# A graph-convolution kernel: the last unit takes the first two row tiles of g from SBUF instead of gathering them

## The chip, the cores and the metric

The kernel runs on one NeuronCore of one Trainium2 chip. The metric is the device time of one launch in microseconds, as the median of several runs. The inputs are fixed: the adjacency matrix always has the same pattern of zeros, so the sizes of all lists below are the same in every run.

## The reference

```python
# x: (8, 4096, 256), adj: (4096, 4096), W: (256, 256), all float32
HW = einsum('bnf,fo->bno', x, W)
A = relu((adj + adj.T) * 0.5)                 # sparse: most entries are 0
D = A.sum(1);  d = where(D > 0, D ** -0.5, 0)
out = relu(einsum('nm,bmo->bno', I - d[:, None] * A * d[None, :], HW))
result = layernorm(x + out)                   # over the last axis, eps 1e-5
```

An entry of adj off the diagonal is nonzero with a probability that falls with row and column number, so the first rows of A are the densest.

## The kernel before, in words

*Stage one* symmetrises adj in blocks of 512, writes A with an altered diagonal to a tensor in DRAM (`a_dram`), forms g = d * x * W (one row of g has all 8 batches, 2048 numbers or 8 KB) and writes it to `g_dram`. It also marks, for every row of A and every group of 32 columns, whether the row has any entry there (`uses`). Row tile 0 of the output is computed in this stage.

*Stage two* computes the other 31 row tiles of 128 rows, in units: unit u makes row tiles 2u+1 and 2u+2, its two blocks, and unit 15, the last, only row tile 31. The order of units is `SEQ`. Most rows of A have no entry in a given block, so a unit does not multiply with all 4096 rows. From the marks the kernel builds lists on the device (`patterns`, `place`, `index`, on VectorE, with a few small products on TensorE): which rows have entries in which of the eight groups of 32 columns. A list is cut into tiles of 128 entries, in two halves of 64 slots. `FIRST` and `CAPS` say for each unit and each kind of row (one group only, several groups, and so on) at which half the kind's slots begin and how many halves it has; the number of list tiles of a unit follows from them. A row of a one-group kind that finds no slot goes to a kind for several groups; a row that finds none at all would send the whole program into a slow branch with dense products, which these inputs do not reach.

For each list tile two indirect DMAs on GpSimd's queue (L951, L959) gather the entries of A (tile `ga`, 128 rows by 32, 128 or 256 columns) and the rows of g (tile `g`, 128 by 2048, 1 MB; rows of g are skipped for blank slots). They go into a ring of 12 slots, in the order of first use; a slot is refilled when TensorE has used its tile for the last time.

The first two row tiles of g, where A is dense, are kept in SBUF for the whole stage (`g_hub`, the hub tiles). `HUBS[u]` says how many of them unit u uses. `patterns` clears the marks of these rows (L262), so they do not enter the unit's lists. What they need is only a 128 by 128 piece of A for each block (`gh`), loaded with a plain DMA on GpSimd's queue by `load_hub_rows` as soon as the unit before has used its own.

Products are in *steps* (`steps_of`). A full step multiplies one 128 by 128 piece with 2048 columns of g: four matmuls of 512 columns into four PSUM banks. A tiled step uses TensorE as eight tiles of 64 by 32: `REACH` or `RING` list tiles are looked at, and for each bank up to eight products of different halves and column groups run at once. After the products of each bank of a tiled step, an empty instruction on ScalarE (L1201, a "tick") marks that they are done, and two banks later TensorE waits for it[...]. Tiles of rows with several groups in one block take a full step.

Behind the products of a block, `finish` evicts its four banks on ScalarE (L767), and VectorE adds x (L777), takes the statistics (L786, L788), forms the inverse root (L799 to L805) and scales (L810); SyncE stores. Row tile 31 has its own version, `finish_last`, which works in four quarters of two batches: evictions on ScalarE (L1016), adds on GpSimd (L1024, L1037) and VectorE (L1026, L1032), statistics on VectorE, the power on GpSimd (L1039), the scaling on ScalarE (L1048), four stores (L1055). The x it needs is loaded into the first ring slot that is free when all gathers have been asked for (L979). The order on each queue is the order in which the program is written: `queue(...)` ties a new instruction behind the last one of that engine, and `after(n, ...)` puts a piece of work some steps later.

The last unit before: `HUBS[15]` is 0, its list has ten tiles, and its steps are: one full step with list tile 8; two tiled steps with tiles 0, 2, 4, 6 and 1, 3, 5, 7, eight products a bank; one tiled step with tile 9, four products a bank. Unit 14 before it takes 11 steps; the last two are full steps of row tile 30 (hub tile 1 and a list tile), and the two before those are tiled steps in which row tile 29 ends.

Of the kernel before, what the change touches and what calls it, by code (L numbers as in the profile page):

```python
# [22 lines left out]

SEQ = [*range(1, 10), 0, *range(10, 16)]

HUBS = [*[2] * 15, 0]

CAPS = [
    [3, 4, 3, 3, 3, 2, 3, 3, 2, 3, 3, 3, 3, 3, 11],
# [11 lines left out]
    [2, 2, 2, 2, 3, 3, 3, 2, 2, 1, 1, 1, 1, 1, 1],  # L41
    [2, 2, 2, 2, 2, 2, 2, 2, 2, 2, 1, 1, 1, 1, 1],
    [2, 2, 2, 2, 2, 2, 2, 2, 2, 2, 1, 1, 1, 1, 1],
    [3, 4, 4, 4, 4, 0, 0, 0, 0, 0, 0, 0, 0, 0, 0],
]

FIRST = [
# [12 lines left out]
    [0, 2, 6, 4, 8, 16, 12, 21, 19, 15, 24, 28, 26, 25, 27],  # L60
    [2, 4, 6, 8, 0, 16, 18, 10, 14, 12, 20, 22, 21, 24, 23],
    [2, 6, 0, 4, 8, 14, 10, 16, 12, 18, 22, 24, 23, 20, 21],
    [16, 0, 4, 8, 12, 20, 20, 20, 20, 20, 20, 20, 20, 20, 20],
]


# [1 line left out]
def kernel(  # L68
# [49 lines left out]
    def blocks(u):  # L118

        return min(2, NB - 1 - 2 * u)  # L120
# [75 lines left out]
    singles, pairs, whole = slice(1, 1 + NE), slice(10, 14), slice(0, 10, 9)  # L196
# [28 lines left out]
    for s in range(NE):  # L225
        h = slice((s % QU) * E, (s % QU + 1) * E)
# [16 lines left out]
    def patterns(u):  # L243

        def t(shape, name, dtype=F32, **kw):
            return ipool.tile(shape, dtype, tag=name, name=f"{name}_{u}", **kw)
# [13 lines left out]
        nc.vector.tensor_tensor(diag, diag, own[:, :, :nb], ALU.max)  # L260
        if HUBS[u]:
            nc.vector.memset(used[:, :, : HUBS[u]], 0.0)  # L262
        several = t([P, NB], "several", bufs=1)
# [206 lines left out]
    with (  # L470
# [71 lines left out]
        held = {}  # L542
# [155 lines left out]
        for i in range(NS):  # L698
# [35 lines left out]
            if i in (1, 2, 3, 4):  # L734
                u = SEQ[i - 1]
# [6 lines left out]
            if i in (2, 4):  # L742
                u = SEQ[i // 2 - 1]
# [82 lines left out]
    def steps_of(u):  # L826

        kind_at = {}
        for k, kind in enumerate(KINDS):
            for s in range(FIRST[u][k], FIRST[u][k] + CAPS[u][k]):  # L830
                kind_at[s] = kind
        every = 255 if blocks(u) == 2 else 15
        whole = {0: [], 15: [], 240: []}
        todo = []
        for t in range(tiles[u]):
            pair = kind_at.get(2 * t), kind_at.get(2 * t + 1)
            if pair[0] == pair[1] and pair[0] in whole:
                whole[pair[0]].append(t)
                continue
            todo.append(  # L840
                [
                    (t, i, b, j)
                    for b in range(2)
                    for i, kind in enumerate(pair)
                    for j in range(QU)
                    if kind is not None and (kind or every) >> QU * b + j & 1
                ]
            )
        rounds = []
        while any(todo):  # L850
            todo = [ops for ops in todo if ops]
            taken = {}
            for ops in todo[: REACH if blocks(u) == 2 else RING]:
                for op in ops:
                    taken.setdefault((op[1], op[3]), op)
            rounds.append(list(taken.values()))
            todo = [[op for op in ops if op not in rounds[-1]] for ops in todo]
        n = len(rounds)
        first_b1 = min([r for r in range(n) if any(op[2] for op in rounds[r])], default=n)
        last_b0 = max([r for r in range(n) if any(not op[2] for op in rounds[r])], default=-1)  # L860

        def full(t, b):
            return [(t, None, b, None)]

        def weave(*several):
            several = [list(s) for s in several]
            total = [len(s) for s in several]
            out = []
            while any(several):
                at = max(range(len(several)), key=lambda k: (len(several[k]) / max(total[k], 1), total[k]))  # L870
                out.append(several[at].pop(0))
            return out

        held = range(HUBS[u])
        out = [full(-1, 0)] if HUBS[u] else []
        starts = [full(t, 0) for t in whole[15]]
        if not out and starts:
            out.append(starts.pop(0))
        out += weave(rounds[:first_b1], [full(-1 - h, 0) for h in held[1:]], starts)
        if blocks(u) == 1:  # L880
            return out + [full(t, 0) for t in whole[0]]
        out += [full(-1, 1)] if HUBS[u] else []
        rows = [[full(t, 0), full(t, 1)] for t in whole[0]]
        between = [[r] for r in rounds[first_b1 : max(last_b0 + 1, first_b1)]]
        out += chain.from_iterable(weave(between, rows))
        out += weave(
            [full(-1 - h, 1) for h in held[1:]],
            [full(t, 1) for t in whole[240]],
            rounds[max(last_b0 + 1, first_b1) :],
        )  # L890
        return out

    with (
# [5 lines left out]
            gath.enter_context(tc.tile_pool(name=f"hub_{h}", bufs=1)).tile([P, G], F32, name=f"g_hub{h}")  # L899
            for h in range(max(HUBS))  # L900
        ]
# [8 lines left out]
        lpool = gath.enter_context(tc.tile_pool(name="spread", bufs=1))  # L910
        stat = gath.enter_context(tc.tile_pool(name="stat", bufs=3))
        steps = [(u, step) for u in SEQ for step in steps_of(u)]
        order = list(dict.fromkeys((u, op[0]) for u, step in steps for op in step if op[0] >= 0))
        uses_left = {}
# [12 lines left out]
        def queue(engine):  # L927

            traced = reversed(nc.cur_bb.bb.instructions)
            return tc.issue_after(next(i for i in traced if i.engine == engines[engine]))  # L930

        def load_hub_rows(units, h, b):

            u = next((v for v in units if HUBS[v] > h), None)
            if u is None:
                return
            i = 2 * u + 1 + b
            with queue("pool"):
                nc.gpsimd.dma_start(
                    hub_rows[h][b], a_dram[h * P : (h + 1) * P, i * P : (i + 1) * P]  # L940
                )
            got[u, -1 - h, b] = (hub_rows[h][b], hubs[h], 0, False)
# [53 lines left out]
        u = SEQ[0]  # L996
        xr = {i: residual(i, nc.sync) for i in (0, *range(2 * u + 1, 2 * u + 1 + blocks(u)))}
        for h in range(max(HUBS)):
            with queue("pool"):
                nc.gpsimd.dma_start(hubs[h], g_dram[h * P : (h + 1) * P, :])  # L1000
            for b in range(2):
                load_hub_rows(SEQ, h, b)
# [201 lines left out]
        for q, (u, step) in enumerate(steps):  # L1204
# [26 lines left out]
            if step[0][1] is None:  # L1231
                (op,) = step
                b = op[2]
# [15 lines left out]
            for op in step:  # L1249
                t = op[0]  # L1250
                uses_left[u, t] -= 1
                if t < 0:
                    load_hub_rows(SEQ[SEQ.index(u) + 1 :], -1 - t, op[2])
# [74 lines left out]
```

## Time and profile before

| what | value |
|---|---|
| timed runs | 1494.57, 1494.57, 1493.09 us; median 1494.57 |
| profiled execution | 1742.82 us, span 1740.8 us |
| TensorE, VectorE, GpSimd, ScalarE busy | 84%, 60%, 43%, 21% of the span |
| mean granted TensorE clock | 0.916 |
| transfers | 543 MB, mean 312 GB/s |
| gathers | 268 of `ga` and 268 of `g`, 1.03 and 1.11 us of GpSimd each |
| last unit's products | 1704.9 to 1719.1 us of the span |

The profiled execution is 248 us longer than a timed one, so its times are compared with each other, and a difference in them with a difference of medians. "Busy" of TensorE counts a matmul from its start to a modelled end. In a line of the timeline the columns are start, duration, engine, line, operation, output and inputs with shapes and count, and in brackets the engine's idle time before it and what ended it; a matmul in float32 shows as two records. In the chain of work, each piece is named with its start, duration, engine and line, as found by following what released what, back from the last instruction.

### The profile page before, as it was taken

To read this page: it belongs to the slowest core of one execution; us is meant where nothing else is said; L and a number is where in the kernel's file an instruction comes from. 1 tells how busy PE (TensorE), PEld (TensorE's weight loads), DVE (VectorE), ACT (ScalarE), POOL (GpSimd) and SP (SyncE) were. 2 spreads that over 40 slices of the span, in tenths; PEclk is the share of its full clock that TensorE was granted. 3 is DMA by queue.
4 is the path that set the end of the run, shared out by engine and by line. 5 is a ranking of instruction groups with operands and counts; after the bars stand their busy time and mean duration, and the time that the engine had idled before them with its cause. 6 is when DMAs were issued, how large, how long until landed. Compare 5 with 4: busy or idle time off the path is not lost.

```text
span 1740.8 us, 29689 instructions
## 1 busy us (share of the span) xinstructions
PE 1454.0 (84%) x11008; PEld 736.6 (42%) x11008; DVE 1044.4 (60%) x3173; ACT 361.0 (21%) x462; POOL 752.6 (43%) x1564
## 2 busy tenths in 40 slices
PE   7999989899999879879687777876878987797784
PEld 6777777667776323223222222221323332232221
DVE  5675688887875400819183764946748036867446
ACT  4555554445545000000001010010110010011002
POOL 2442010121323663445455645446456346556652
PEclk9999999999999889989888988988879998998987
DMA  9999999999999996868786968879779559769983
GB/s 350 353 368 393 401 354 390 368 339 355 341 374 395 370 347 215 323 223 300 257 297 248 344 231 336 297 250 323 254 262 331 223 202 362 294 245 358 371 321 113
DMA packets 217159, 543.04 MB, mean 312 GB/s; under 512 B 19369, under 2 KB 109193, under 8 KB 182425
## 3 DMA queue, kind: packets, MB, share of 16 engines
q0 software_dynamic: 55664, 283.87, 43.7%
q1 hardware_dynamic: 93472, 126.89, 21.3%
q10 hardware_dynamic: 67872, 130.32, 19.8%
q8 instruction: 89, 1.46, 0.3%
q14 instruction: 62, 0.51, 0.1%
HBM read 438.03 MB, written 136.34 MB: 330 GB/s over the span
## 4 chain that ended last, share of the span: by engine, by line
PE 55%; another core or an unknown queue 14%; DVE 12%; DMA 10%; issue 5%; POOL 2%; ACT 2%; ACTq 0%; DVEq 0%; POOLq 0%
PE py L1166 37%; PE pg L606 8%; DMA a_dram<-sym 5%; PE lead L564 3%; PE xtr L595 3%; PE tr L495 3%; DVE sym L499 3%; DMA xin<-in_x_dram 2%; DMA ga<-a_dram,ai 1%; DVE stats L786 1%; DVE xr L810 1%; POOL g L959 1%; DVE sums L506 1%; POOL ga L951 1%
## 5 line engine op out<-in xcount | busy, mean ns | idle before, releaser
L1166 PE MATMUL py<-g,ga 64*32 64x512 f32 (+1 forms) x7136 | 686.7, 664 | 214.4 <-ACTq L1201 188.0
L1166 PEld LDWEIGHTS py<-g,ga 64*32 64x32 f32 (+1 forms) x7136 | 212.5, 120 | 669.3 <-ACTq L1201 351.3
L951 POOL DMA_INDIRECT ga<-a_dram,ai x268 | 275.5, 1028 | 286.8 <-PE py L1166 219.6
L959 POOL DMA_INDIRECT g<-g_dram,gi x268 | 296.8, 1108 | 171.5 <-PE py L1166 85.6
L767 ACT ACTIVATE y<-py,minus_r 128x512 f32<-128x512 f32 x120 | 72.8, 688 | 1048.8 <-PE py L1166 928.2
L442 DVE TENSOR_SCALAR low<-lists 128x17 f32<-128x17 f32 (+8 forms) x14 | 2.5, 176 | 436.1 <-PE lists L430 352.9
L606 PE MATMUL pg<-w_sb,xt 128*128 128x256 f32 x1024 | 229.7, 383 | 4.3 <-ACT xt L596 4.3
L1166 PE MATMUL py<-g_hub,gh 128*128 128x512 f32 x480 | 223.8, 608 | 6.4 <-DVE pos_k L239 6.4
L606 PEld LDWEIGHTS pg<-w_sb,xt 128*128 128x128 f32 x1024 | 194.7, 193 | 30.8 <-ACT xt L596 5.2
L499 DVE TENSOR_TENSOR sym<-tr,adj 128x512 f32<-128x512 f32 x256 | 162.7, 683 | 56.8 <-PE tr L495 38.9
L506 DVE TENSOR_REDUCE sums<-sym 128x64 f32<-128x2048 f32 x64 | 145.3, 2279 | 63.3 <-ACT sym L503 63.3
L495 PE MATMUL tr<-ident,adj 128*128 128x128 f32 x1024 | 136.1, 280 | 21.0 <-DVE sym L499 14.9
L1166 PEld LDWEIGHTS py<-g_hub,gh 128*128 128x128 f32 x480 | 88.9, 192 | 139.0 <-issue 124.4
L503 ACT ACTIVATE sym<-sym 128x2048 f32<-128x2048 f32 x64 | 122.6, 1915 | 114.6 <-DVE sym L499 102.2
L495 PEld LDWEIGHTS tr<-ident,adj 128*128 128x128 f32 x1024 | 115.4, 143 | 53.4 <-DVE sym L499 32.7
L507 POOL TENSOR_SCALAR uses<-sums 128x64 uint8<-128x64 f32 x64 | 24.9, 388 | 239.2 <-DVE sums L506 203.1
L777 DVE TENSOR_TENSOR xr<-xr,y 128x2048 f32<-128x2048 f32 x31 | 70.9, 2287 | 57.6 <-ACT y L767 57.6
L595 PE MATMUL xtr<-ident,xin 128*128 128x128 f32 x512 | 76.2, 301 | 18.6 <-DVE sym L499 11.9
L810 DVE TENSOR_SCALAR xr<-xr,mv,root 128x256 f32<-128x256 f32 x248 | 87.0, 422 | 1.1
L786 DVE BATCH_NORM_STATS2 stats<-xr 128x6 f32<-128x256 f32 x248 | 84.1, 412 | 1.1
L564 PE MATMUL lead<-gt,strip 128*128 128x512 f32 x176 | 83.2, 593 | 0.0
L596 ACT COPY xt<-xtr 128x512 f32<-128x512 f32 x128 | 68.1, 592 | 60.2 <-PE xtr L595 59.2
(157 smaller groups left out, 1060.6 us busy)
## 6 DMA issues: line engine op xcount, KB each, us to landing
adj<-in_adj_dram SPq DMA_DIRECT2D x64, 1024.0 KB
a_dram<-sym ACTq DMA_DIRECT2D x64, 1024.0 KB
out_dram<-xr SPq DMA_DIRECT2D x31, 1024.0 KB
xr<-in_x_dram ACTq DMA_DIRECT2D x28, 1024.0 KB
xin<-in_x_dram SPq DMA_DIRECT2D x44, 512.0 KB
g_dram<-gt ACTq DMA_DIRECT2D x22, 1024.0 KB
xin<-in_x_dram POOLq DMA_DIRECT2D x20, 512.0 KB
g_dram<-held ACTq DMA_DIRECT2D x10, 1024.0 KB
```

The lines of the kernel that those rows point to most:

```text
L495: ins = nc.tensor.transpose(pt[:, c * P : (c + 1) * P], tji[:, c, a * P : (a + 1) * P], ident)
L499: nc.vector.tensor_add(sym[:, a, :], pt, tij[:, a, :])
L503: nc.scalar.activation(sym, sym, AF.Relu, scale=0.5)
L506: nc.vector.tensor_reduce(sums, sym.rearrange("p a (c q) -> p a c q", q=E), AX.X, ALU.add)
L564: nc.tensor.matmul(lead[c], lhsT=strip, rhs=g[:, c * S : (c + 1) * S], start=not done, stop=len(done) == NB - 1, skip_group_check=True,)
L595: nc.tensor.transpose(pt[:, k, c, :], xin[b // H][:, b % H + k, c * P : (c + 1) * P], ident)
L606: ins = nc.tensor.matmul(pg[:, k * FO : (k + 1) * FO], lhsT=xt[:, b + k, c, :], rhs=w_sb[:, c, :], start=(c == 0), stop=(c == FC - 1),)
L786: nc.vector.bn_stats(stats[:, b, :], z[:, b, :])
L810: nc.vector.tensor_scalar(z[:, b, :], z[:, b, :], mv[:, b, 0:1], rstd[:, b : b + 1], ALU.subtract, ALU.mult,)
L951: nc.gpsimd.indirect_dma_start(out=at if both else at[:, : E if one else P], out_offset=None, in_=a_pairs if both else a_groups if one els ...
L959: nc.gpsimd.indirect_dma_start(out=gt, out_offset=None, in_=g_dram, in_offset=bass.IndirectOffsetOnAxis(ap=gi[:, t : t + 1], axis=0), boun ...
L1166: return nc.tensor.matmul(py[2 * u + 1 + b][c][cols, :], lhsT=at[ps, off + cols.start : off + cols.stop], rhs=gt[ps, c * S : (c + 1) * S], ...
```

## The change

The last unit uses the two hub tiles like every other unit. Its lists then leave out the first 256 rows and shrink from ten tiles to seven: three halves instead of four for each one-group kind, two instead of three for rows with several groups. In `steps_of`, a unit with one block puts its second hub tile and its full steps ahead of its tiled steps, where they were woven before. `load_hub_rows` asks for a unit that has the block, since the last unit has only block 0.

```diff
-HUBS = [*[2] * 15, 0]
+HUBS = [2] * 16

 CAPS = [
...
-    [3, 4, 4, 4, 4, 0, 0, 0, 0, 0, 0, 0, 0, 0, 0],
+    [2, 3, 3, 3, 3, 0, 0, 0, 0, 0, 0, 0, 0, 0, 0],

 FIRST = [
...
-    [16, 0, 4, 8, 12, 20, 20, 20, 20, 20, 20, 20, 20, 20, 20],
+    [12, 0, 3, 6, 9, 14, 14, 14, 14, 14, 14, 14, 14, 14, 14],

@@ steps_of
+        if blocks(u) == 1:
+            return out + [full(-1 - h, 0) for h in held[1:]] + starts + rounds + [full(t, 0) for t in whole[0]]
         out += weave(rounds[:first_b1], [full(-1 - h, 0) for h in held[1:]], starts)
-        if blocks(u) == 1:
-            return out + [full(t, 0) for t in whole[0]]

@@ load_hub_rows
-            u = next((v for v in units if HUBS[v] > h), None)
+            u = next((v for v in units if HUBS[v] > h and blocks(v) > b), None)
```

The last unit's steps after: hub tile 0, hub tile 1, list tile 6 (three full steps); a tiled step with tiles 0 to 5, eight products a bank; a tiled step with tiles 1, 2, 4 and 5, four products a bank.

## The prediction

> **What bounds the kernel now.** I read the page's first line and its chain of work first, to see how much of the profiled time exists in a timed run at all, then the chain in order of time over the last 60 us, then the timeline and the table of stretches there. The page:
>
> ```profile
> span 1740.8 us, 29689 instructions
> ...
> PE 55%; another core or an unknown queue 14%; DVE 12%; DMA 10%; issue 5%; POOL 2%; ACT 2%; ACTq 0%; DVEq 0%; POOLq 0%
> ```
>
> The profiled execution took 1742.82 us, 2.0 us of them outside the span; the median of the timed runs is 1494.57. The 248 us between them are almost exactly the 14% (244 us) that the chain books to waits with no known cause. I take those waits for something that the timed runs don't have; that is argued from two numbers that agree, not shown. In the last unit and behind it the chain has none of them, so a difference made there carries over to the median as it is. The chain in order of time (start, duration, what):
>
> ```profile
> 1688.13 9.94 PE py L1166 x128
> ...
> 1698.25 2.43 ACT y L767 x4
> ...
> 1700.70 2.31 DVE xr L777
> ...
> 1711.63 2.21 DVE xr L777
> ...
> 1720.12 4.24 DVE xr L810 x7
> 1724.36 0.60 DVE g L1026
> ```
>
> From 1698.25 the end is not set by TensorE. The two tiled steps that close row tile 29 (unit 14) end; ScalarE evicts row 29; VectorE does rows 29 and 30 one after the other (1700.7 to 1724.3), and only then the adds, statistics and scaling of row 31, the last unit. That last unit's products run beside this (timeline, then stretches: us, busy time of each engine, clock, DMA share, GB/s):
>
> ```profile
> 1703.59 15.32 PE L1166 MATMUL py<-g,ga 128*128 128x512 f32 x171
> 1719.12 2.42 ACT L1016 ACTIVATE y<-py,minus_r 128x512 f32<-128x512 f32 x4 [13.36 <-DVE half L804]
> 1719.79 4.57 DVE L810 TENSOR_SCALAR xr<-xr,mv,root 128x256 f32<-128x256 f32 x8
> 1719.90 1.43 POOL L1024 TENSOR_TENSOR g<-g,y 128x512 f32<-128x512 f32 x1 [18.41 <-ACT y L1016]
> 1721.29 1.30 POOL L1037 TENSOR_TENSOR g<-g,y 128x512 f32<-128x512 f32 x1
> 1724.28 0.68 DVE L1026 TENSOR_TENSOR g<-g,y 128x512 f32<-128x512 f32 x1
> ```
>
> ```profile
> 1656.60:1704.90 48.30, 40.13 (x362) 14.68 (x362) 20.74 (x77) 4.76 (x8) 23.63 (x24) 0.89 0.82 306
> 1704.90:1719.10 14.20, 14.01 (x169) 4.89 (x167) 13.34 (x59) 0.73 (x2) 0.00 (x0) 1.00 0.30 102
> ```
>
> The second stretch is the last unit: four steps in 14.2 us, TensorE busy for 14.0 at full clock. No gather holds it: the semaphores in the trace show its last two tiles of g landed at 1700.8 and 1702.0, while the steps that use them start near 1711.8 and 1715.2. So TensorE has cover. Quarter 1 of row 31 is evicted by 1720.4 (1719.71 + 0.68) and VectorE takes it at 1724.28: 3.9 us. Quarter 0 is summed on GpSimd by 1721.32 and VectorE turns to it at 1724.88: 3.6 us.
>
> **What the Trainium skill says.** "SBUF — State Buffer", section "Who interferes with whom": VectorE and GpSimd share a port pair, held for a whole instruction; a VectorE operation with two inputs in SBUF, or in a two-port mode, and a GpSimd operation that reads SBUF block each other. The trace agrees for L810: two of its eight took 1.35 us instead of 0.40, beside L1024 and L1037. "TensorE: Matmul & The Clock Gate", section "What's actually happening": after an idle window of about 3.4 us the array runs at half clock. The trace agrees: after gaps of 2.6 and 4.7 us in unit 14 the granted clock was 0.50 in 1678-1680 and 1688-1692. "TensorEngine Tiling (Array Packing)", section "Key Properties": tiles of the array work independently. So a tiled step should cost what its fullest tile costs, not the number of its products; agreed below.
>
> **The change, part by part.** A step is four banks of 512 columns. A full step starts 3.43 us before the next (1663.73 to 1667.16), a tiled one of eight products takes the same, and the last unit's third tiled step, with four products a bank, also took 0.86 us a bank.
>
> *Products.* Before: one full step, two tiled steps of eight products a bank, one of four; four steps. After: the hub tiles 0 and 1 of g (full), the full step of list tile 6, a tiled step of eight and one of four; five. Full products rise from 4 to 12, tiled ones fall from 80 to 48, but time counts steps: 5 x 3.43 against 4 x 3.43, +3.4 us on TensorE. The four products left in the last step sit on four different tiles of the array, so it isn't shorter.
>
> *Gathers.* Three of ten tiles fall away: on GpSimd 3 x (0.95 + 1.01 + two gaps of 0.30) = 7.7 us, less two hub loads of rows of A, 0.59 each: -6.5 us. These are off the path: GpSimd itself waits on TensorE here (4.12 us before the gather of 1694.87). The slots hold fewer blanks: counted from the inputs, 987 rows of A have an entry in the last block, 838 without the first 256; 149 x 8 KB = 1.2 MB less, 3 us of transfer at the 400 to 430 GB/s of 1670-1690, against 0.13 MB for the hub loads. Nothing waited for them, so 0. The hub loads stand in GpSimd's queue behind the first and third step of unit 14, each ahead of a gather that waits for the step after it; nobody waits longer. The load of x for row 31 moves ahead of unit 14's last tiled steps; it was not awaited before.
>
> *Lists.* One VectorE memset more, four GpSimd memsets less, eight small VectorE operations and 32 products narrower (together those products took 0.95 us). All run in earlier units under the waits of VectorE (24.3 us before L442): 0.
>
> *Sum on the path.* TensorE ends 3.43 us later, near 1722.3, so L1024 runs 1723.33-1724.76. VectorE, no longer held by L1024 and L1037, finishes row 30 at about 1722.4 instead of 1724.28 and takes quarter 1 when it is evicted, 1723.8. L1026 has two SBUF inputs and now falls under L1024: if it is held until 1724.76 it ends near 1725.4, and the statistics of quarter 0 start 0.5 us later than before (1724.88). If the two don't block, 0; if L1037 gets the pair first as well, another 1.3, so 1.9. I take +0.5: the blocked L810 got its turn between the two GpSimd adds. Span 1741.3, profiled run 1743.3, median 1494.57 + 0.5 = 1495.1 us.
>
> **Rivals.** *Faster: the tail of a timed run waits for gathers.* Without the unexplained waits TensorE asks sooner. The 31.8 MB moved in 1607.9-1704.9 took 97 us; TensorE was busy for 78.4 of them, which would ask for 405 GB/s, about what saturated stretches reached. So the last tiles may come late in a timed run though the profile shows 11 us of room. Then a landing sets the end: before, that of list tile 7, the ninth gathered, two steps from the end (tile 9 takes only blanks: the 123 rows with several groups fit tile 8); after, that of tile 5, the seventh, also two steps from the end. It comes sooner by 1.1 MB at 405 GB/s, 2.7 us, or, if GpSimd's issue is the limit, by 2 x 2.56 - 1.2 = 3.9 us; and a wait that puts one step at half clock costs the old order up to 3.4 more. Middle of -2.7 and -7.3: -5.0, 1489.6 us. Against it: rows 29 and 30 on VectorE still end 26 us after row 29's products, so the old order must have been late by over 3.6 us before anything is gained.
>
> *Slower: the cover is gone.* One mechanism: TensorE's extra step stands in the open. The cover of 3.6 us is eaten when the last unit starts later against VectorE's rows 29 and 30, for example because unit 14's last two full steps or the hub steps run at half clock (+3.4 us for each such step). It decides from 0.1 us of lost cover on, and by 3 us or more it costs 3.4 + 0.5: 1498.5 us. For it: the mean clock of 0.89 in the first stretch means a fifth of it at half clock. Against it: the clock was 1.0 from 1694 on.
>
> *The lists don't hold.* A row without a slot would send the program into the full branch, over 4096 products of 0.86 us, 3.5 ms. The count excludes it: 204, 188, 189 and 177 rows with one group against 192 slots each, 12 over; with 80 rows of several groups that makes 92 for the 128 slots of list tile 6.
>
> **How the numbers follow.** Within 0.2% (3 us, about what can be told from no change) is the first case and small parts of both rivals: 0.50. Faster 0.31 is the gather rival, slower 0.19 the lost cover. The first case alone reaches from 1492 (2.7 us of bytes) to 1497 (1.9 and rounding up). For 8 in 10 the range takes in most of both rivals: 1488.0 to 1499.0, which leaves out the far end of the gather rival and two half-clock steps in the open.
>
> **What would show it.** Right: in the profile after, five steps of 3.4 us between row 30's last product and L1016, L1016 about 24 us after row 29's first eviction instead of 20.9, row 30's L810 without the 1.35 us pieces, L1026 waiting for ScalarE or GpSimd instead of following L810, and the stretch from row 29's eviction to the end within 1 us of 42.6. Wrong: waits of TensorE inside the last unit; a last step of less than 3.4 us; row 29's eviction itself earlier against the start of unit 14, which nothing here should move. Most likely to break it: timed runs in which TensorE is not where the profile has it.

## The result, and the profile after

The changed kernel took 1487.32 us (median of 7 runs, 1483.71 to 1490.79), the kernel before 1493.09 us (7 runs, 1490.74 to 1494.58) in the same comparison: a ratio of 0.9959 with a 95% interval of 0.994 to 0.9978, so 3 to 9 us faster. The forecast was 1495.1 us, no measurable change. In a later comparison the ratio was 0.9974 (0.9962 to 0.9987).

One thing has to be known to read all that follows: in some comparisons every execution of the kernel before took 1485 to 1501 us (kind A), in others 1710 to 1746 us (kind B). Its two profiles of kind B have 13 and 14% of waits of unknown cause in their chain of work, its profile of kind A has none. What makes the kind isn't known; it isn't the chip alone, for the chip numbered 10 in the record was of kind A in one comparison and of kind B in a later one. The profile shown ahead of the prediction is of kind B, the times that it was to explain are of kind A. A ratio is always against runs of the kernel before in the same comparison. The changed kernel itself was timed in kind A alone.

The profile of the changed kernel is of kind A. Its page (first line, then the shares of the chain of work) has no waits of unknown cause:

```profile
span 1488.3 us, 29574 instructions
...
PE 53%; DMA 23%; DVE 16%; issue 5%; ACT 2%; POOL 1%; ACTq 0%; DVEq 0%; POOLq 0%
```

The profiled execution took 1490.79 us. The 244 us really are absent where the kernel takes 1490 us, and 23% of the chain are transfers instead of 10%. The chain in order of time (start, duration, what) over the last 105 us:

```profile
1383.79 33.45 DMA out_dram<-xr
...
1417.33 31.87 DMA xr<-in_x_dram
1449.20 1.94 DVE xr L810 x6
1451.13 8.62 issue
1459.76 2.30 DVE xr L777
...
1468.34 4.24 DVE xr L810 x7
1472.57 0.60 DVE g L1026
```

The last work is held by VectorE as in the forecast, but not for its reason. Rows 29 and 30 don't follow each other: VectorE stands idle for 8.6 us until x of row 30 is there. ScalarE asked for it at 1417.33, and the last packets of ScalarE's queue moved at 1459.1, 42 us later; the median of these loads is 15.1 us. The timeline of the same stretch (start, duration, engine, line, what, and in brackets the idle time before it):

```profile
1440.76 3.60 PE L1166 MATMUL py<-g,ga 128*128 128x512 f32 x8
...
1444.19 7.03 PE L1166 MATMUL py<-g_hub,gh 128*128 128x512 f32 x16
...
1451.06 4.58 PE L1166 MATMUL py<-g,ga 128*128 128x512 f32 x14
...
1458.40 9.99 PE L1166 MATMUL py<-g,ga 64*32 64x512 f32 x90 [2.75 <-DMA g<-g_dram,gi]
1459.76 2.29 DVE L777 TENSOR_TENSOR xr<-xr,y 128x2048 f32<-128x2048 f32 x1 [8.62 <-issue]
...
1468.01 4.57 DVE L810 TENSOR_SCALAR xr<-xr,mv,root 128x256 f32<-128x256 f32 x8
1468.57 2.42 ACT L1016 ACTIVATE y<-py,minus_r 128x512 f32<-128x512 f32 x4 [23.49 <-PE py L1166]
1469.34 1.49 POOL L1024 TENSOR_TENSOR g<-g,y 128x512 f32<-128x512 f32 x1 [21.17 <-ACT y L1016]
```

The five steps are there, the two hub steps first. TensorE then waits for a gathered tile of g inside the last unit, which the prediction had named as the sign that it is wrong, and the two tiled steps behind the wait take 9.99 us instead of 6.9. The table of stretches (us, busy time of TensorE, its weight loads, VectorE, ScalarE and GpSimd, granted clock, DMA share, GB/s) for the steps of unit 14 and for the last unit shows why:

```profile
1396.00:1437.22 41.22, 41.22 (x440) 16.18 (x424) 21.61 (x81) 4.84 (x8) 27.70 (x26) 1.00 1.00 375
1444.19:1468.40 24.21, 21.44 (x121) 8.79 (x119) 14.60 (x65) 0.89 (x2) 3.34 (x4) 0.86 0.63 236
```

In unit 14 the DMA engines are busy for the whole time at full clock of TensorE; in the profile before they had been busy for 0.82 of it, at a mean clock of 0.89. The transfers of the last unit start with a backlog that the stretched execution didn't have.

### The profile page after: what moved, and what is told of

Same layout as the page of the kernel before. It is cut to its first block, busy times and chain, and to the rows that moved or that the text cites. A ratio compares the mean times of both kernels' runs of the same rounds, so it can differ in the third digit from the quotient of the medians.

```text
span 1488.3 us, 29574 instructions
## 1 busy us (share of the span) xinstructions
PE 1381.5 (93%) x10960; PEld 749.5 (50%) x10960; DVE 1042.9 (70%) x3174; ACT 360.8 (24%) x462; POOL 761.4 (51%) x1556
## 4 chain that ended last, share of the span: by engine, by line
PE 53%; DMA 23%; DVE 16%; issue 5%; ACT 2%; POOL 1%; ACTq 0%; DVEq 0%; POOLq 0%
PE py L1166 33%; PE pg L606 9%; DMA g<-g_dram,gi 7%; DMA a_dram<-sym 6%; DVE sym L499 3%; PE lead L564 3%; PE tr L495 3%; PE xtr L595 3%; DMA xin<-in_x_dram 3%; DMA out_dram<-xr 2%; DMA xr<-in_x_dram 2%; DMA ga<-a_dram,ai 2%; DVE stats L786 2%; DVE xr L810 1%; DVE xr L777 1%
## 5 line engine op out<-in xcount | busy, mean ns | idle before, releaser
L1166 PE MATMUL py<-g,ga 64*32 64x512 f32 (+1 forms) x7072 | 612.4, 610 | 23.1 <-DMA g<-g_dram,gi 22.0
L1166 PEld LDWEIGHTS py<-g,ga 64*32 64x32 f32 (+1 forms) x7072 | 226.8, 114 | 392.1 <-issue 314.7
L951 POOL DMA_INDIRECT ga<-a_dram,ai x265 | 282.9, 1068 | 136.2 <-PE py L1166 64.1
L1166 PE MATMUL py<-g_hub,gh 128*128 128x512 f32 x496 | 229.2, 604 | 3.8 <-DVE pos_k L239 3.8
L495 PEld LDWEIGHTS tr<-ident,adj 128*128 128x128 f32 x1024 | 115.2, 143 | 53.7 <-DVE sym L499 32.5
L595 PE MATMUL xtr<-ident,xin 128*128 128x128 f32 x512 | 72.8, 291 | 21.3 <-DVE sym L499 12.3
L810 DVE TENSOR_SCALAR xr<-xr,mv,root 128x256 f32<-128x256 f32 x248 | 87.6, 425 | 1.1
## 6 DMA issues: line engine op xcount, KB each, us to landing
xr<-in_x_dram ACTq DMA_DIRECT2D x28, 1024.0 KB, 15.1
```

The lines of the kernel that those rows point to most:

```text
L495: ins = nc.tensor.transpose(pt[:, c * P : (c + 1) * P], tji[:, c, a * P : (a + 1) * P], ident)
L595: nc.tensor.transpose(pt[:, k, c, :], xin[b // H][:, b % H + k, c * P : (c + 1) * P], ident)
L810: nc.vector.tensor_scalar(z[:, b, :], z[:, b, :], mv[:, b, 0:1], rstd[:, b : b + 1], ALU.subtract, ALU.mult,)
L951: nc.gpsimd.indirect_dma_start(out=at if both else at[:, : E if one else P], out_offset=None, in_=a_pairs if both else a_groups if one els ...
L1166: return nc.tensor.matmul(py[2 * u + 1 + b][c][cols, :], lhsT=at[ps, off + cols.start : off + cols.stop], rhs=gt[ps, c * S : (c + 1) * S], ...
```

## The experiments

The theories, as the expectations name them. **T1**: the end waits for x of row 30, which lands late beside the gathers. **T2**: it waits for the last awaited tile of g, through TensorE and L1016. **T3**: what sets that landing is the number of list tiles (GpSimd's issue), not the bytes. **T4**: the order of the steps is what gains.

### The kernel before, profiled twice more

> The kernel before, unchanged: one more look at its tail, for a profile that is not stretched by waits of unknown cause. If the tail of a timed run waits for transfers (T1: x of row 30 lands late beside the gathers; T2: a tile of g for the last unit lands late), this profile shows either VectorE idle between rows 29 and 30 until x of row 30 lands, later than the 8.6 us seen in the changed kernel, or TensorE waiting for g inside the last unit. If the profile on record was right about the tail, rows 29 and 30 follow each other on VectorE without a gap, and neither theory holds.

This execution took 1719.58 us and repeats the profile before: 13% of unknown waits, rows 29 and 30 end to end. It says nothing on kind A.

> The kernel before, unchanged, a third look: the two profiles on hand are of executions over 1700 us, with 13 to 14% of waits of unknown cause, while the times of the comparison are near 1491 us. If this execution is of the second kind, T1 expects VectorE idle for more than 8.6 us before row 30 (x of row 30 lands late) and T2 TensorE waiting for g in the last unit; the forecast's reading expects neither.

This one took 1486.7 us, so it is of kind A (the "second kind" of the expectation). Its last unit (timeline):

```profile
1430.41 2.42 ACT L767 ACTIVATE y<-py,minus_r 128x512 f32<-128x512 f32 x4 [30.78 <-PE py L1166]
...
1443.84 5.66 PE L1166 MATMUL py<-g,ga 64*32 64x512 f32 x60 [2.21 <-DMA g<-g_dram,gi]
...
1450.73 1.02 PE L1166 MATMUL py<-g,ga 64*32 64x512 f32 x2 [1.24 <-DMA g<-g_dram,gi]
1451.99 2.29 DVE L777 TENSOR_TENSOR xr<-xr,y 128x2048 f32<-128x2048 f32 x1 [8.12 <-issue]
1453.83 1.38 PE L1166 MATMUL py<-g,ga 64*32 64x512 f32 x2 [2.08 <-DMA g<-g_dram,gi]
1456.79 9.20 PE L1166 MATMUL py<-g,ga 64*32 64x512 f32 x90 [1.58 <-DMA g<-g_dram,gi]
...
1460.24 2.67 DVE L810 TENSOR_SCALAR xr<-xr,mv,root 128x256 f32<-128x256 f32 x8
...
1466.17 2.42 ACT L1016 ACTIVATE y<-py,minus_r 128x512 f32<-128x512 f32 x4 [28.24 <-PE py L1166]
...
1467.47 1.28 DVE L1026 TENSOR_TENSOR g<-g,y 128x512 f32<-128x512 f32 x1 [4.56 <-ACT y L1016]
```

TensorE waits four times for g in the last unit. The last of these gathers is the first piece of the chain of work behind it (start, duration, what):

```profile
1444.45 12.20 DMA g<-g_dram,gi
...
1456.79 9.22 PE py L1166 x90
```

The last awaited tile lands 26.4 us after row 29's first eviction (1456.8 - 1430.4), and L1016 comes 35.8 us after it, where the profile before had 20.9. VectorE has done row 30 by 1462.9 and is idle for 4.56 us before L1026: here the gathers set the end (T2). x of row 30 is late as well (VectorE's 8.12 us), and about as late: VectorE begins row 30 21.6 us after row 29's eviction here and 22.2 us after it in the changed kernel. What differs is TensorE's end.

Two stretches make these profiles comparable: from unit 14's first hub step, and from row 29's first eviction (R29), to the end. All rows of this table are profiles of kind A; the ratios are those of the timed runs.

| kernel | first hub step to end | R29 to end | R29 to L1016 | R29 to end of row 30 | GpSimd's last drain | ratio |
|---|---|---|---|---|---|---|
| before | 87.4 | 54.3 | 35.8 | 32.5 | 8.74 | 1 |
| changed | 82.6 | 50.7 | 31.0 | 35.0 | 8.32 | 0.9959, 0.9974 |
| ten tiles, hubs | 88.3 | 56.2 | 37.6 | 33.9 | 8.81 | 1.0006 |
| nine tiles, no hubs | 84.3 | 51.0 | 32.7 | 32.2 | 8.48 | 0.9991 |
| changed, old order | 85.7 | 51.7 | 33.8 | 31.2 | 8.32 | 0.9989 |
| before, x of row 30 moved | 85.2 | 52.0 | 36.3 | 24.4 | 0.73 | 0.9984 |
| changed, x of row 31 split | 80.7 | 48.8 | 31.0 | 35.1 | 0.73 | 0.9961 |
| changed, x of row 30 moved | 80.8 | 47.1 | 31.4 | 24.5 | 0.73 | 0.9966, 0.9951 |

### Tiles or bytes: the hub tiles with the old list of ten tiles

```diff
-    [2, 3, 3, 3, 3, 0, 0, 0, 0, 0, 0, 0, 0, 0, 0],
+    [3, 4, 4, 4, 4, 0, 0, 0, 0, 0, 0, 0, 0, 0, 0],
...
-    [12, 0, 3, 6, 9, 14, 14, 14, 14, 14, 14, 14, 14, 14, 14],
+    [16, 0, 4, 8, 12, 20, 20, 20, 20, 20, 20, 20, 20, 20, 20],
```

> The changed kernel with the old sizes of the last unit's lists: the hub tiles are used and the first 256 rows are gone from the lists (838 rows of g instead of 987), but the 838 rows lie in ten tiles, and there are six steps instead of five. T1 (bytes: x of row 30 lands when the gathers have drained): 1.2 MB are saved as in the change, so most of the 6 us gain stays, less what a sixth step of 3.4 us puts in the open: 1487 to 1491. T2 (the last g tile's landing sets TensorE's end): the last tiled steps wait for tiles 7 and 9, the gain shrinks to about 2 us: 1490 to 1492. T3 (GpSimd's issue, 2.56 us a tile): the ten tiles are asked for as late as before, nothing is gained: 1493 or more.

> The changed kernel with its 838 rows spread over ten list tiles and six steps. If bytes decide (T1, T2 by bytes), the last landing comes as early as in the changed kernel and only the sixth step is added at TensorE's end, 3.4 us less 3 us of slack: a ratio to before of 0.996 to 0.997. If the number of tiles decides (T3, each tile costs GpSimd two issues and the queue a turn), three more tiles cost 2.6 to 3.3 us each, and nothing is left of the gain: 1.000 to 1.003.

The first run was of kind B (0.9994, 0.9975 to 1.0013). The second, of kind A: 1.0006 (0.9992 to 1.0021). Nothing is left of the gain, though the same 838 rows are gathered. Its timeline:

```profile
1443.87 7.03 PE L1166 MATMUL py<-g_hub,gh 128*128 128x512 f32 x16
...
1465.06 9.62 PE L1166 MATMUL py<-g,ga 64*32 64x512 f32 x90 [2.08 <-DMA g<-g_dram,gi]
1474.87 2.42 ACT L1016 ACTIVATE y<-py,minus_r 128x512 f32<-128x512 f32 x4 [29.52 <-PE py L1166]
```

The last wait ends 27.8 us after row 29's eviction (at 1437.2), against 20.8 in the changed kernel and 26.4 before: with ten tiles the awaited one lands as late as ever, with the rows spread thinner. So the number of tiles sets the landing, which is T3's main claim. The awaited gather in the chain of work of this profile:

```profile
1452.57 12.36 DMA g<-g_dram,gi
```

From the start of its issue to its landing it takes 12.4 us, as in the kernel before (12.20) and in the changed kernel, where it is issued at 1446.21 and the wait ends at 1458.40. So what moves the landing is when the gather is issued: 14.0 us after row 29's eviction before, 8.6 in the changed kernel, 15.4 here. The time of an issue by itself is only part of the reason for that: in the kernel before, the last eight gathers of g are issued 3.5 us apart on average (1423.35 to 1447.88), not 2.56, and GpSimd's waits between them are mostly for earlier gathers to land. The sixth step isn't what costs: it stands ahead of the last wait, and what is behind it is the same in both kernels, 90 records in 9.62 and 9.99 us.

### One tile and one step less, without hub tiles

```diff
-    [3, 4, 4, 4, 4, 0, 0, 0, 0, 0, 0, 0, 0, 0, 0],
+    [2, 4, 4, 4, 4, 0, 0, 0, 0, 0, 0, 0, 0, 0, 0],
...
-    [16, 0, 4, 8, 12, 20, 20, 20, 20, 20, 20, 20, 20, 20, 20],
+    [16, 0, 4, 8, 12, 18, 18, 18, 18, 18, 18, 18, 18, 18, 18],
```

> The kernel before without its tenth list tile, which holds only blanks: no hub tiles in the last unit, 987 rows of g in nine tiles, three steps instead of four. T1 (bytes): the rows are the same, so no change: 1492 to 1494. T2: the tile of the last step is one that is needed anyway, and one step of 3.4 us goes: up to 3.4 us faster, 1490. T3 (GpSimd's issue): one tile of 2.56 us less, 1490.5. My forecast's reading (VectorE sets the end, gathers and products are hidden) also says no change.

> The kernel before without its tenth list tile of blanks: 987 rows in nine tiles, three steps, no hub tiles. T2 with TensorE's end as the bound: the step behind the last landing goes, L1016 comes 3.4 us sooner, and VectorE's row 30, which ended 3.3 us before L1016, then sets the end: 3 us faster, a ratio of 0.998. T1 (row 30 sets the end): no change but for 0.3 us of drain, 0.9995 to 1.000. If the number of tiles decides the last landing, it doesn't move either, since the tenth tile is gathered behind the awaited ones.

In kind B 1.0003 (0.9985 to 1.0021), as the forecast's reading would have it there. In kind A 0.9991 (0.9979 to 1.0002): half of what T2 expected, not excluding it and not telling it from no change. The profile is clearer: the last wait ends where it did (26.3 us), TensorE is done 3.1 us sooner, and L1026's wait for L1016 falls from 4.56 us to

```profile
1470.75 1.28 DVE L1026 TENSOR_TENSOR g<-g,y 128x512 f32<-128x512 f32 x1 [1.88 <-ACT y L1016]
```

The stretch from row 29's eviction is 3.3 us shorter. By these profiles, then, a step behind the last landing is in the open, and the sixth step of the kernel with ten tiles, ahead of it, was free.

### The old order of steps

```diff
-        if blocks(u) == 1:
-            return out + [full(-1 - h, 0) for h in held[1:]] + starts + rounds + [full(t, 0) for t in whole[0]]
         out += weave(rounds[:first_b1], [full(-1 - h, 0) for h in held[1:]], starts)
+        if blocks(u) == 1:
+            return out + [full(t, 0) for t in whole[0]]
```

> The changed kernel with its five steps in the old order: hub tile 0, first tiled step, hub tile 1 and the full list tile, second tiled step, so that a tiled step that needs gathered tiles comes second and not fourth. T1 (x of row 30 sets the end through VectorE): the same bytes, so the same gain, 1487 to 1488. T2 and T4 (the gathers' landing sets TensorE's end, and full steps ahead of it cover the wait): TensorE waits at its second step for the tiles that it now awaits at its fourth, with two full steps of 3.4 us still to come, which fall behind the wait: up to 7 us lost, 1490 to 1494.

> The changed kernel with the old order of steps: hub tile 0, first tiled step, hub tile 1, full list tile, second tiled step. T2: TensorE waits for the tiles of the first tiled step as long as before, and now has three steps of 3.4 us behind the wait instead of one; its last product ends some 3 to 7 us later than in the changed kernel, of which about 3 us were slack behind row 30: 0 to 4 us are lost, a ratio to before of 0.996 to 0.999. If only the rows that are no longer gathered matter, the ratio is that of the change, 0.996.

In kind B 0.9969 (0.9949 to 0.9988), in kind A 0.9989 (0.9976 to 1.0003). Against the two ratios of the change that is a loss of 2 to 4.5 us from the order alone, but the intervals overlap and the two kernels weren't timed side by side. The timeline of the latter:

```profile
1453.84 5.54 PE L1166 MATMUL py<-g,ga 64*32 64x512 f32 x58 [5.88 <-DMA g<-g_dram,gi]
...
1459.31 3.70 PE L1166 MATMUL py<-g_hub,gh 128*128 128x512 f32 x8
1462.85 7.16 PE L1166 MATMUL py<-g,ga 128*128 128x512 f32 x40
```

The wait is 5.88 us instead of 2.75, ends 3.4 us sooner (17.4 us after row 29's eviction: the ring is filled in the order of first use, so the six awaited tiles are gathered ahead of the full one), and three steps stand behind the waiting step instead of one. L1016 comes 2.8 us later than in the changed kernel, as T2 and T4 have it: the new order puts the steps that need no gather under the wait. Less of it reaches the end of the kernel, 0.9 us (51.7 against 50.7 us from row 29's eviction), because in the changed kernel VectorE comes to L1026 late, from row 30. What the order is worth there is not settled.

### x of row 30 on GpSimd's queue

```diff
-                with queue("act"):
-                    xr[i] = residual(i, nc.scalar)
+                with queue("pool" if i == NB - 2 else "act"):
+                    xr[i] = residual(i, nc.gpsimd if i == NB - 2 else nc.scalar)
```

> The changed kernel with one load moved: x of row 30 is asked for on GpSimd's queue, ahead of the last unit's gathers, and no longer on ScalarE's queue beside them. T1 (in the changed kernel x of row 30, which landed 42 us after it was asked for, holds VectorE and so the end): x lands within 15 us, VectorE ends row 30 near 4 us before the last evictions instead of 3 us after them, and the end is then set by TensorE: 1.5 to 3 us faster than the changed kernel, a ratio to before of 0.992 to 0.995. T2 alone (the landing of g sets the end, x doesn't matter): the gathers stand behind one more megabyte, 0 to 2.5 us slower than the changed kernel, a ratio of 0.996 to 0.998.

> The kernel before with the same load moved. In the kernel before TensorE's wait for g sets the end and VectorE has 4.6 us to spare after row 30, so T2 expects no gain, and up to 2.5 us of loss where the gathers stand behind the megabyte: a ratio of 1.000 to 1.002. T1 for the kernel before (x of row 30 sets its end as well) expects 1 to 3 us of gain: 0.998 to 0.999.

0.9966 (0.9951 to 0.9982) for the changed kernel with the load moved, 0.9984 (0.997 to 0.9997) for the kernel before with it. The second lies in the range that T1 gave for it, but not by T1's mechanism: L1016 comes 0.5 us later, as T2 has it, and yet the end comes 2.3 us sooner after row 29's eviction. The reason isn't row 30, which VectorE ended before L1016 in either kernel. All instructions of the last line, where the engines meet, by GpSimd (count; shortest, median and longest in ns; first and last start), first in the kernel before, then with the load moved:

```profile
L1323 POOLq DRAIN  x3: 46/103/8737, 1475.1 to 1484.4; - x3
```

```profile
L1323 POOLq DRAIN  x3: 46/103/726, 1483.0 to 1489.4; - x3
```

In the kernels before and after, GpSimd's last drain takes 8.3 to 8.8 us and ends 2.1 to 2.8 us behind every other engine (before, 1483.85 against SyncE's 1481.04); the chain of work doesn't show it, since a drain isn't counted as work. With the load moved it takes 0.73 us. The next experiment separates the two effects.

### The drain alone: x of row 31 in two loads

```diff
-                with queue("pool"):
-                    nc.gpsimd.dma_start(
-                        xr[NB - 1], x[:, (NB - 1) * P :, :].rearrange("b p f -> p b f")
-                    )
+                for fs in (slice(0, F // 2), slice(F // 2, F)):
+                    with queue("pool"):
+                        nc.gpsimd.dma_start(
+                            xr[NB - 1][:, :, fs], x[:, (NB - 1) * P :, fs].rearrange("b p f -> p b f")
+                        )
```

> The changed kernel itself, on the same chip as the next three, as their measure. The ratio of the comparison was 0.9959; 0.994 to 0.998 is expected whatever the cause.

> The changed kernel with the load of x of row 31 cut into two loads of half the columns each on GpSimd's queue: the same bytes, twice the pieces, row 30 untouched. If GpSimd's last drain depends on how many pieces its queue has had, it falls from 8.3 to about 0.7 us as with the moved load, and the end comes about 2.1 us sooner (0.0014 below the changed kernel), while row 30 still ends late. If the drain fell because row 30's load moved away from ScalarE's queue, it stays at 8.3 us and the time is the changed kernel's.

> The changed kernel with x of row 30 on GpSimd's queue, beside the changed kernel on the same chip. If row 30's x and GpSimd's last drain (8.32 us in the changed kernel, 0.73 us in the first run of this one) both stand in the end, the tail is 3.7 us shorter, as in the profiles (47.1 against 50.8 us from row 29's eviction): 0.0025 below the ratio of the changed kernel. If the landing of g alone sets the end: equal to the changed kernel, within 0.001.

All side by side, in kind A: the changed kernel 0.9974 (0.9962 to 0.9987), with x of row 31 split 0.9961 (0.9944 to 0.9977), with x of row 30 moved 0.9951 (0.9936 to 0.9965). Against the changed kernel, means of 13 to 22 runs, the split is 1.9 us faster (-0.6 to 4.2), the moved load 3.4 us (1.5 to 5.3). The split brings the drain to

```profile
L1324 POOLq DRAIN  x3: 46/103/726, 1485.5 to 1492.2; - x3
```

with row 30 as late as ever (35.1 us). So the drain falls with what is put on GpSimd's queue, not with row 30. In the kernel with the moved load (its second profile), row 30 is early and TensorE sets the end:

```profile
1446.45 2.28 DVE L777 TENSOR_TENSOR xr<-xr,y 128x2048 f32<-128x2048 f32 x1
...
1465.74 1.28 DVE L1026 TENSOR_TENSOR g<-g,y 128x512 f32<-128x512 f32 x1 [8.38 <-ACT y L1016]
```

L1026 comes 32.9 us after row 29's eviction instead of 34.9, and the stretch to the end is 47.1 to 47.3 us against 48.8 with the split alone. By the profiles, then, T1 holds for the changed kernel and is worth 1.6 us; the times of these two kernels alone leave it open (1.6 us, -1.0 to 4.1).

> The changed kernel with x of row 30 on GpSimd's queue, again, beside the split load. If row 30's late x holds the end of the changed kernel (T1), this kernel is 1.7 us faster than the one with the split load (0.0011 in the ratio), as the profiles have it (47.1 against 48.8 us from row 29's eviction to the end); if the drain is all, the two are equal.

> The changed kernel with the load of x of row 31 in two pieces, again: a ratio of 0.996 if the first run's 0.9961 was right, and 0.0011 above the kernel with the moved load if row 30's x counts.

> The kernel before with the load of x of row 31 cut into two loads. Its last drain took 8.74 us and ended 2.85 us behind all other engines, so if the drain falls to 0.73 us as in the changed kernel, the end comes about 2.8 us sooner: a ratio of 0.998. If the moved load's gain in the kernel before (0.9984) came from row 30's x, nothing changes here: 1.000.

These three were of kind B: 0.9966 (0.9946 to 0.9986), 0.9977 (0.9952 to 1.0002), and 0.9985 (0.9963 to 1.0007) for the kernel before with x of row 31 split. There row 30 begins 13.3 us after row 29's eviction with and without the moved load, so the two were to be equal if T1's reason is right, and their medians are (1721.50 and 1721.32); the wide intervals make that weak support. The drain fell from 8.74 to 0.82 us in the kernel before too; its stretch from row 29's eviction to the end is 2.8 us shorter in the profile (39.8 against 42.6 us), as expected. The ratio of 0.9985 agrees with that but doesn't tell it from no change; the two medians are equal (1725.5 us).

### Products that fill the wait

```diff
+                if blocks(u) == 1 and steps[q - 1][1][0][1] is None:
+                    warm = psum.tile([P, S], F32, tag="b1", name="warm")
+                    for n in range(8):
+                        with queue("pe"):
+                            nc.tensor.matmul(
+                                warm, lhsT=hub_rows[0][0], rhs=hubs[0][:, :S], start=n == 0, stop=n == 7
+                            )
                 tiled(u, step, last)
```

> The kernel with the moved load, and eight products of a hub tile of 0.43 us each ahead of the last unit's first tiled step, into a bank that nothing reads: they fill 3.4 us in which TensorE waited for g (3.2 to 3.5 us). If the clock of 0.71 in the two tiled steps behind the wait comes from the wait, they take 7 us instead of 10, less up to 0.3 us by which the extra products overrun: 2.5 to 3 us faster than the kernel with the moved load, a ratio 0.0018 lower. If the clock doesn't follow from the wait, equal.

> The changed kernel with the moved load and eight products of a hub tile ahead of the last unit's first tiled step, again. Where TensorE waits 3.2 to 3.5 us for g there and the two tiled steps behind it take 10 us at a clock of 0.71, they should take about 7 us now, so a ratio of about 0.994 (0.9951 and 0.9966 without the products). Where the kernel before takes over 1700 us, TensorE doesn't wait in the last unit, and the eight products cost up to 3.4 us: 0.998 to 1.001.

Both were of kind B, 1.001 (0.9984 to 1.0036) and 1.0018 (0.9994 to 1.0042), and the expectation was wrong by a factor of two: a product of 512 columns takes 0.86 us, its two records 0.43 each, so eight take 6.9 us, and the profile shows just that between the full step and the first tiled one (6.8 us). There it is lost time: L1016 comes 31.2 us after row 29's eviction, against 24.3 in the kernel with the moved load in kind B. Whether a full clock could be had behind the wait stays open.

## Why the prediction was wrong

**The failed step** is the one on gathers: three tiles fewer, "Nothing waited for them, so 0." In the kernel before, in kind A, TensorE did wait for them, four times in the last unit, and the landing of the last awaited tile set TensorE's end and with it the kernel's. With three tiles fewer that landing came 5.6 us sooner, where the prediction had put 0. Behind it stands the choice to let a difference in the last unit of the profiled execution "carry over to the median as it is". The 244 us of waits were rightly taken as absent from the timed runs; but a stall of TensorE isn't neutral for what comes after it. That these stalls gave the transfers time to catch up, and made the 11 us of room at the last tiles, is the likeliest reading, not shown by an experiment: in the profile of kind B the DMA engines were busy for 0.82 of unit 14, in the same kernel's profile of kind A for the whole of it (1387 to 1430).

**Products.** Five steps against four, +3.43 us on TensorE: the steps came as counted. But TensorE ended 4.8 us sooner after row 29's eviction (30.8 against 35.6), because the added full steps lie ahead of the last wait: that wait ends 5.6 us sooner, and the steps behind it take 0.8 us longer. "TensorE has cover" of 3.6 us was the reverse of the truth in the executions that were timed: there VectorE had 4.56 us to spare, and TensorE none.

**Gathers.** The bound that the rival gave, 2.7 us by bytes or 3.9 by issue, was of the right kind and too small: the last awaited landing moved from 26.4 to 20.8 us after row 29's eviction, 5.6 us for two tiles fewer ahead of it. The other half of that rival, up to 3.4 us for half clock in the old order alone, was wrong: the steps behind the last wait took 9.20 us before and 9.99 after. Its change of -5.0 us lies beside the measured -5.8 all the same; the mechanism was there, and too little chance was put on it, but that the size fits is in part luck, the sum of a landing that was too small and a half-clock term that was wrong. The argument set against it, that VectorE's rows 29 and 30 end 26 us after row 29's products, failed too: they ended 32.5 us (before) and 35.0 us (changed) after it. x of row 30 was late in both, so VectorE began the row 21.6 and 22.2 us after the eviction instead of 13.3; in the changed kernel the scaling of row 30 also took 4.57 us instead of 2.67.

**Sum on the path.** Of the 4.8 us between the profiles (87.4 to 82.6): 1.2 us lie before row 29's eviction, and this is no scatter. From unit 14's first hub step to that eviction the three kernels without hub tiles in the last unit take 33.1 to 33.3 us, the changed kernel 31.9 and 32.0 in its two profiles. TensorE's records agree to 0.02 us for the first 24 us; then the kernel before waits for a tile of g in a tiled step of unit 14 (its weight loads are idle for 1.10 us, and the product of 1423.06 is released by that landing), and the changed kernel doesn't. So a fifth wait went. Why isn't settled: with hub tiles and ten list tiles it is gone too (32.1 us), and in the changed kernel with the old order, or with x of row 30 moved, the stretch is longer again (34.0 and 33.6). 2.2 us are L1026's earlier start (37.1 to 34.9 us after the eviction): TensorE gave 4.8, and row 30, now the later of the two, took back 2.6. 0.7 us come between L1026 and GpSimd's last power, for here L1026 takes 0.68 us where it took 1.28 beside L1024. That is the predicted +0.5 us with the other sign: row 30's scaling still bears the blocked pieces (4.57 us for eight), and L1026 comes after them. 0.7 us come from GpSimd's last power to the end of its drain, 0.42 of them the drain itself (8.74 to 8.32), on which the prediction had no term.

**What was right.** The count of rows against slots (no row without a slot), the steps, and GpSimd's shorter list. That the work moved in the lists is hidden isn't shown: unit 14's first hub step starts anywhere from 1397 to 1412 us in the profiles of kind A.

**Signs and range.** L1016 was to come about 24 us after row 29's first eviction and the end 42.6 us after it; they came at 31.0 and 50.7. Two of the signs that the prediction had named for being wrong came: TensorE's wait in the last unit, and row 29's eviction earlier against the start of unit 14, by the 1.2 us above. Of those for being right, row 30's scaling without its long pieces and L1026 no longer behind L810 didn't come. The result lies 0.7 us below the range, whose lower end left out "the far end of the gather rival".

**Slower rival.** Cover didn't vanish through half clock in unit 14: the clock was 1.00 from 1396.00 to 1437.22.

**What the experiments give.** Fewer list tiles are needed: the hub tiles without them give 1.0006, clear of the change's 0.9959 and 0.9974. That the order is needed is likely, not shown: without it 0.9989, with an interval that overlaps. And 0.4 us of the gain are GpSimd's shorter drain. The kernel with x of row 30 moved is the fastest of all here: beside the changed kernel's 1487.49 us it took 1484.18.

## What to carry to other kernels

Where a profiled execution is longer than the timed ones by waits of unknown cause, its room on transfers need not be there in a timed one: before calling a gather hidden, work out what rate the transfers would need if the engine that waited didn't, and if that is the rate of the saturated stretches, count the landing as the bound. In a last unit that waits for gathered data, put the work that needs none ahead of the wait and count only what stands behind the last landing. See what the engines do after their last work as well: an engine's drain can end the kernel and be in no chain.

## What the runs showed of the hardware

- **A load starved beside gathers.** In the changed kernel, from 1440 to 1452, GpSimd's queue moved 0.58 to 0.69 MB in each 2 us and ScalarE's queue 0.05 to 0.07, so x of row 30 took 42 us for 1 MB. The Trainium skill, "DMA: Bandwidth & Descriptors", section "Queues, rings and completion order", says that each DMA engine takes turns between queues by packets. That agrees in direction: the rows of g come in pieces of 8 KB, x in pieces of 1 KB. Turns weren't equal in number, though: in these 12 us GpSimd's queue moved 661 pieces, ScalarE's 326 and SyncE's 349.
- **GpSimd's last drain**: 8.74 us with ten list tiles (8.81 with hub tiles besides), 8.48 with nine, 8.32 with seven, and 0.73 to 0.82 where one more load of 1 MB, or the same load in twice the pieces, went over its queue. That it depends on what the queue has had is shown; on what measure of it, isn't.
- **Half clock after a wait.** In the changed kernel TensorE waited for 2.75 us and then ran at a clock of 0.50 from 1458 to 1464. In the kernel before, waits of 1.2 to 2.2 us, one after another, brought the clock to 0.50 as well (1455.5 to 1460); one of 2.21 us alone was enough for 0.50 from 1445 to 1446.5. The skill's "TensorE: Matmul & The Clock Gate", section "What's actually happening", names an idle window of about 3.4 us for the fall to half clock and at least one such window of busy time for the way back. The 6 us fit the second; the waits that were enough for the first were shorter, and so was the gap of 2.6 us in which the prediction saw the trace agree; its gap of 4.7 us does agree.
- **Two kinds of executions.** In kind B, in the second profile of the kernel before, 159 intervals between the ticks of tiled steps are longer than 1.3 us instead of 0.86 (those over 8 us, with other steps between, left out), 341 us in excess, and 224 are shorter than 1 us; GpSimd is issuing transfers for 61% of the long ones and 20% of the short. In kind A the shares are 69% and 65%, and only 30 are long. That tiled products stall in kind B while GpSimd issues gathers is suggested by this, not shown; why the changed kernel with the old order of steps came to 0.9969 there wasn't settled either.
